# A graph layer over 64 samples: weights loaded on ScalarE's queue and combined between the first sample's products, and a third buffer for the token rows

## The chip, the cores and the metric

The kernel runs on one NeuronCore of a Trainium2 chip. TensorE (PE in the profile) multiplies matrices, VectorE (DVE), ScalarE (ACT) and GpSimd (POOL) work elementwise, and SyncE (SP) issues DMAs. Each engine takes its instructions in the order in which they were written, and waits at an instruction until what it needs is there. The metric is the device time of one execution in microseconds (us), lower is better. Times given are medians of several runs, beside one execution taken by the profiler.

## The reference

`x` holds 64 samples of 256 tokens by 768 features, `adj` 64 matrices of 256 by 256 with values 0 and 1. Cut to what matters, for each sample:

```python
h = relu((x - mean(x)) / sqrt(var(x) + 1e-5))
deg, rdeg = adj.sum(-1), adj.T.sum(-1)
ctx = adj @ (h @ Wadj.T + badj) / max(deg, 1)
ctx += adj.T @ (h @ Wrev.T + brev) / max(rdeg, 1)
ctx += h @ Wself.T + bself
rel = (adj-weighted sum of E[rels]) @ Wr.T + br * deg
rel += (the same, transposed) @ Wrr.T + brr * rdeg
out = x + ctx + rel
```

All of it is float32. The relation numbers are the entries of `adj` itself, so with entries 0 and 1 the sums over `E` reduce to one row of `E` times a degree. Should `adj` hold anything else, a general path behind a flag computes the sample again; with this input it isn't entered.

## The kernel before

**The products.** For one sample the left side has six blocks of 128 tokens by 768 features: `a0, a1, a2` for the first 128 tokens and `b0, b1, b2` for the last 128, where 0 is the aggregate over `adj`, 1 the aggregate over its transpose, and 2 the sample's own features. The right side has nine blocks of 768 by 256: `Wadj`, `Wrev` and `Wself` (first digit 0, 1, 2), each in three column blocks (second digit). Instead of the 18 block products, 15 are made, in the manner of fast matrix multiplication: `PRODUCTS` gives for each the combination of left blocks and of right blocks, and `ORDER` (line 62) the order in which they run, the PSUM bank each adds to, a row product that brings in the biases, which output blocks read the bank afterwards and with which sign, and which left combinations GpSimd has to form ahead. A product is six matmuls of 128x128 by 128x256 over the feature blocks (L333; the profile shows each as two instructions, x12 for a product), and five products have a row product behind them (L338), whose left side is `tokT`, the token rows of the sample: degrees and flags, transposed. Banks `x` and `y` have a buffer each; `w`, `z`, `v`, `u` and `t` take turns in two buffers of one pool, so that `z` of one step takes over the buffer that `t` of the step before had.

**The stages of a sample.** `load` brings in `x`, `adj` and the transposed `x` (three DMAs on SP). `degrees` converts `adj` on ScalarE and sums its rows. `statistics` gives mean, variance (VectorE, with the power -0.5 on GpSimd) and the degrees' reciprocals into `cols`. `spread` transposes `cols` on TensorE into `pt`; ScalarE copies it as `tokT` (L262) and as `line` (L264); `line` goes by two DMAs to DRAM (`d`) and comes back broadcast over all partitions as `row`. `normalise` makes `hx` on VectorE (L282), its upper part `hi` on ScalarE (L285) and the remainder `lo` on VectorE (L286), for each half of the tokens. `self_features` scales the transposed `x` by `row` in two GpSimd passes (L298) and takes its positive part on ScalarE (L299), which is left block 2. `aggregate` multiplies `hi` and `lo` with `adj` for one feature block (`pa`, L307), and VectorE scales the result into left blocks 0 and 1 (`X`, L312). `combine_left` (L328) forms a sum or difference of left blocks on GpSimd. `add_out` (L346 and L348) adds a bank to, or takes it from, the output that grows in the tile `x`, on VectorE.

**The order of the work.** Nothing is scheduled automatically: each engine's order is the order of the calls. `step(t)` (L350) runs the 15 products of sample M = t. Between them stand the six aggregates of A = t + 1 (after products 2 to 7) and its `self_features`, and for N = t + 2 the degrees and statistics (after the seventh), `spread` (after the tenth) and `normalise` (after the twelfth). At the end of the step GpSimd forms the first three left combinations of A, and the output of M leaves in one DMA of 768 KB.

**The buffers.** `tokT` comes from a pool of two (L261). `tokT` of N is written in step M after the tenth product, into the buffer of sample M, which the row products of M read up to the fifteenth.

**The start.** The steps -2 and -1 have no products. In step -2, after the loads of sample 0, `load_weights` (L150) issues 15 DMAs of 768 KB on SP, one weight block for each product; `prepare_rows` (L172) loads `eT`, `wr`, and the bias rows behind them on the same queue and builds `rows`, the right side of the row products; `combine_weights` (L156) makes the 15 sums and differences of weight blocks and two sign passes, all on VectorE. Only then does VectorE turn to sample 0's statistics.

**The end.** After the last step a sum over `others` and a tiny matmul give the flag (L398 to L401).

Of the kernel before, what the change touches and what calls it, by code (L numbers as in the profile page):

```python
# [9 lines left out]
F32 = mybir.dt.float32  # L10
F32R = mybir.dt.float32r
# [6 lines left out]
P = 128  # L18
# [4 lines left out]


PRODUCTS = {
    11: ("a1", "-12 +10 +22"),
    10: ("b2-a1", "+22 -11"),
    3: ("a1+b1", "+12 -02 -11"),
    2: ("a2+b2", "+21 -01 -22"),
    5: ("b0+b1", "+10"),  # L30
    9: ("a0+a2", "-20"),
    7: ("a1+a2", "+22"),
    8: ("a1+b0+b1", "+02 -10"),
    6: ("a0+a2+b2", "+20 -01"),
    15: ("b1+b2", "+11"),
    14: ("a0+a1+b0+b1", "-02"),
    12: ("a0+a2+b0+b2", "+01"),
    4: ("b2", "+21 -11 -20"),
    13: ("a0", "-00 +02 +20"),
    1: ("b0", "+00 -01 -10"),  # L40
}

# [12 lines left out]
}  # L55
AHEAD = ("b2-a1", "a1+b1", "a2+b2")

ROWS = ((0, 1, None), (1, 2, None), (0, None, 2), (0, 2, 0), (1, 1, None), (1, 0, 1))

# [10 lines left out]
    (8, "y", None, ((1, 1, 2),), ()),  # L70
    (6, "x", None, ((-1, 0, 1),), ("a0+a1+b0+b1",)),
    (15, "u", None, ((1, 1, 1, 2),), ("a0+a2+b0+b2",)),
    (14, "y", 2, ((-1, 0, 2),), ()),
    (12, "x", 4, ((1, 1, 1),), ()),
    (4, "t", None, ((-1, 0, 1), (1, 1, 1)), ()),
    (13, "y", 3, ((-1, 0, 0),), ()),
    (1, "x", 5, ((1, 1, 0),), ()),
)

# [2 lines left out]
def kernel(  # L82
# [54 lines left out]
    def main_path(main: ExitStack):  # L137
# [12 lines left out]
        def load_weights():  # L150
            for n, (_, right) in PRODUCTS.items():
                k, o = int(right[1]), int(right[2])
                v = (wadj_t, wrev_t, wself_t)[k].rearrange("(f p) o -> p f o", p=P)
                nc.sync.dma_start(W[n], v[:, :, ts(o, NB)])  # L154

        def combine_weights():  # L156
            single = {right[1:]: n for n, (_, right) in PRODUCTS.items() if len(right) == 3}
            for n, (_, right) in PRODUCTS.items():
                first, *others = right.split()
                for k, other in enumerate(others):  # L160
                    w = W[single[other[1:]]]
                    if other[0] == "-":
                        nc.vector.tensor_sub(W[n], W[n], w)  # L163
                    elif first[0] == "-" and k == 0:
                        nc.vector.tensor_sub(W[n], w, W[n])
                    else:
                        nc.vector.tensor_add(W[n], W[n], w)
            for block, n in single.items():
                if PRODUCTS[n][1][0] == "-":
                    nc.vector.tensor_scalar(W[n], W[n], -1.0, None, op0=ALU.mult)  # L170

        def prepare_rows():  # L172


            eT = pool1.tile([P, NREL], F32, name="eT")
            nc.sync.dma_start(eT, e_t)
            wr = [pool1.tile([P, H], F32, tag=f"hl{k}", name=f"wr{k}") for k in range(2)]
            nc.sync.dma_start(wr[0], wr_t)
            nc.sync.dma_start(wr[1], wrr_t)
            brow = pool3.tile([P, H], F32, tag="x", name="brow")  # L180
            nc.vector.memset(brow, 0.0)
            pick = pool1.tile([P, 2, P], F32, tag="t0", name="pick")
            nc.vector.memset(pick, 0.0)
            for q in range(4):
                nc.sync.dma_start(brow[q * 32 : q * 32 + NROW, :], bias)
                nc.vector.tensor_copy(pick[:, 0, q * 32 + 3 : q * 32 + 4], eT[:, 1:2])
                nc.vector.tensor_copy(pick[:, 1, q * 32 + 4 : q * 32 + 5], eT[:, NBASE + 1 : NBASE + 2])
            for n in range(2):
                pr = ps2.tile([P, 512], F32, tag="pa", name=f"pr{n}")
                for k in range(2):  # L190
                    nc.tensor.matmul(pr[:, :HO], pick[:, k, :], wr[k][:, ts(n, HO)], start=(k == 0), stop=(k == 1))
                nc.vector.tensor_add(brow[:, ts(n, HO)], brow[:, ts(n, HO)], pr[:, :HO])
            full = pool3.tile([P, len(ROWS), NB], F32, tag="x", name="rows_full")
            hi = pool1.tile([P, len(ROWS), NB], F32R, tag="hx", name="rows_hi")
            nc.vector.memset(full, 0.0)
            for q in range(4):
                at = slice(q * 32, (q + 1) * 32)
                for k, (c, plus, minus) in enumerate(ROWS):
                    if c != q // 2:
                        continue  # L200
                    if plus is None:
                        nc.vector.tensor_scalar(full[at, k, :], brow[at, ts(minus, NB)], -1.0, None, op0=ALU.mult)
                    elif minus is None:
                        nc.vector.tensor_copy(full[at, k, :], brow[at, ts(plus, NB)])
                    else:
                        nc.vector.tensor_sub(full[at, k, :], brow[at, ts(plus, NB)], brow[at, ts(minus, NB)])
            nc.vector.tensor_copy(hi, full)
            nc.vector.tensor_sub(rows, full, hi.bitcast(F32))
            for q in (0, 2):
                at = slice(q * 32, (q + 1) * 32)  # L210
                nc.vector.tensor_copy(rows[at], hi[at].bitcast(F32))

        S = [{} for _ in range(B)]

# [40 lines left out]
        def spread(b):  # L255

            s = S[b]
            v = cols[b % 2]
            pt = ps1.tile([P, P], F32, tag="pt", name=f"pt_{b}")
            nc.tensor.transpose(pt, v.rearrange("p c k -> p (c k)"), ident)  # L260
            s["tokT"] = pool2.tile([P, P], F32R, tag="tokT", name=f"tokT_{b}")  # L261
            nc.scalar.activation(s["tokT"], pt, AF.Copy)  # L262
# [6 lines left out]
            nc.sync.dma_start(  # L269
                s["row"].rearrange("p k i -> p (k i)"), d.rearrange("k c p -> (k c p)").partition_broadcast(P)  # L270
            )
# [68 lines left out]
        def add_out(b, ps, sign, c, n, many=1):  # L340
# [6 lines left out]
            else:  # L347
                nc.vector.tensor_sub(o, o, ps)  # L348

        def step(t):  # L350

            M, A, N = t, t + 1, t + 2
            has_m, has_a, has_n = 0 <= M < B, 0 <= A < B, 0 <= N < B
            if has_n:
                load(N)
            if t == -2:
                load_weights()
                prepare_rows()
                combine_weights()
            if has_a:  # L360
                new_left(A)
            banks = {}
            for k, (n, bank, row, reads, needs) in enumerate(ORDER):
                if has_m:
                    for name in needs:
                        combine_left(M, name)
                    start = bank not in banks
                    if start:
                        pool, tag = (ps1, bank) if bank in ("x", "y") else (ps2, "q")
                        banks[bank] = pool.tile([P, 512], F32, tag=tag, name=f"{bank}_{M}")[:, :NB]  # L370
                    product(M, n, banks[bank], start, row)
                    for read in reads:
                        add_out(M, banks[bank], *read)
# [15 lines left out]
            if has_m:  # L389
# [5 lines left out]
        for t in range(-2, B):  # L395
            step(t)
        total = pool1.tile([P, 1], F32, name="total")
        nc.vector.tensor_reduce(total, others, AX.X, ALU.add)  # L398
        pf = ps1.tile([P, P], F32, tag="pt", name="pf")
        nc.tensor.matmul(pf[:1, :1], total, ones[:, :1], start=True, stop=True)  # L400
        nc.vector.tensor_copy(flag, pf[:1, :1])  # L401

    def general_path(sub: ExitStack):

# [159 lines left out]
```

## Time and profile before

| | |
|---|---|
| median of 3 runs (lowest, highest) | 3280.49 us (3275.93, 3283.17) |
| profiled execution, its own time | 3272.29 us |
| its span, first to last instruction | 3270.5 us |
| mean granted TensorE clock | 0.975 of full |
| busy: TensorE, GpSimd, VectorE, ScalarE | 91%, 54%, 38%, 10% |
| mean DMA rate | 71 GB/s |

In the rows of the timeline and of the list of groups, `out<-in` are the names in the program; where one line records two instructions of a kind in a row, the count stands behind an x. PE is a matmul, PEld its weight load, SPq SyncE's queue of DMA issues. A row of the windows has, behind the stretch and its length, for PE, PEld, DVE, ACT and POOL the busy time and in brackets the number of instructions, then the granted TensorE clock as a share of full speed, the DMA engines' busy share, and GB/s. What stands as a releaser behind an arrow is what the waiting instruction waited for last.

### The profile page before, as it was taken

What the parts mean: (1) busy time and instruction counts of PE and PEld (TensorE: products, weight loads), DVE (VectorE), ACT (ScalarE), POOL (GpSimd) and SP (SyncE); (2) the same over time, 40 slices, a digit from 0 to 9 for tenths busy, and PEclk for the clock granted to TensorE, in tenths of its full rate; (3) what the DMA queues carried; (4) which work ended last, traced back from release to release, by engine and by line L of the source; (5) the groups of instructions that cost most, each with busy time, mean ns of one, the idle gap of its engine ahead of it and who ended that gap; (6) DMA issues with size and microseconds to landing.
All of it is one profiled execution on the core that took longest, in us unless ns stands there. A gap on an engine that the chain in (4) does not pass through costs nothing.

```text
span 3270.5 us, 33278 instructions
## 1 busy us (share of the span) xinstructions
PE 2972.6 (91%) x13514; PEld 2562.0 (78%) x13514; DVE 1235.7 (38%) x2550; ACT 340.1 (10%) x833; POOL 1771.5 (54%) x902
## 2 busy tenths in 40 slices
PE   0799999999999999999999999999999999999999
PEld 0687877877877877877877877878878778778777
DVE  4533343333333333333333333333333433433332
ACT  0110110110111111101101101101101101101100
POOL 0554654654654654655655655645645546546544
PEclk8899999999999999999999999999999999999999
DMA  5122122122122122222221221221221221221210
GB/s 181 66 83 74 52 84 75 52 75 81 54 75 77 59 75 68 68 74 68 68 75 58 78 75 58 78 74 56 80 74 52 84 75 52 83 75 52 78 65 21
DMA packets 125029, 233.25 MB, mean 71 GB/s; under 512 B 6068, under 2 KB 67252, under 8 KB 124872
## 3 DMA queue, kind: packets, MB, share of 16 engines
q1 hardware_dynamic: 124872, 231.08, 20.4%
q8 instruction: 109, 1.79, 0.2%
q14 instruction: 48, 0.39, 0.0%
HBM read 180.46 MB, written 50.59 MB: 71 GB/s over the span
## 4 chain that ended last, share of the span: by engine, by line
PE 86%; DVE 7%; ACT 4%; SPq 1%; issue 1%; DMA 0%; POOL 0%; ACTq 0%; POOLq 0%
PE y L333 20%; PE x L333 20%; PE z L333 12%; PE pa L307 11%; PE w L333 5%; PE u L333 5%; PE v L333 5%; PE t L333 5%; DVE lo L286 4%; ACT hi L285 3%; DVE hx L282 1%; SPq L154 1%; DVE x L346 1%; DVE x L348 1%; DVE w L163 1%
## 5 line engine op out<-in xcount | busy, mean ns | idle before, releaser
L328 POOL TENSOR_TENSOR b0+b<-X 128x768 f32<-128x768 f32 x64 | 117.2, 1831 | 988.0 <-PE z L333 988.0
L333 PE MATMUL y<-w,X 128*128 128x256 f32 x2304 | 528.6, 379 | 0.0
L333 PEld LDWEIGHTS y<-w,X 128*128 128x128 f32 x2304 | 432.5, 190 | 63.2
L298 POOL TENSOR_TENSOR xT<-xT,row 128x1536 f32<-128x1536 f32 x128 | 441.7, 3451 | 12.0 <-DMA row<-d 6.9
L333 PE MATMUL z<-w,b2-a 128*128 128x256 f32 x768 | 228.9, 460 | 194.2 <-DVE x L346 194.2
L333 PEld LDWEIGHTS z<-w,b2-a 128*128 128x128 f32 x768 | 170.6, 229 | 246.1 <-issue 217.3
L307 PE MATMUL pa<-a,hi 128*128 128x512 f32 x768 | 357.1, 465 | 2.1 <-ACT hi L285 2.1
L328 POOL TENSOR_TENSOR X<-X 128x768 f32<-128x768 f32 x192 | 350.1, 1824 | 10.9 <-PE y L333 5.9
L333 PE MATMUL x<-w,a2+b 128*128 128x256 f32 x1536 | 352.4, 379 | 0.0
L333 PE MATMUL x<-w,X 128*128 128x256 f32 x1536 | 352.3, 379 | 0.0
L312 DVE TENSOR_TENSOR X<-pa,row 128x512 f32<-128x512 f32 x384 | 265.8, 692 | 184.1 <-PE pa L307 182.7
L286 DVE SCALAR_TENSOR_TENSOR lo<-hx,cols,hi 128x768 fp32r<-128x768 f32 x128 | 130.4, 1018 | 507.0 <-ACT hi L285 507.0
L333 PEld LDWEIGHTS x<-w,X 128*128 128x128 f32 x1536 | 286.8, 190 | 40.3
L333 PEld LDWEIGHTS x<-w,a2+b 128*128 128x128 f32 x1536 | 287.2, 190 | 38.0
L307 PE MATMUL pa<-a,lo 128*128 128x512 f32 x768 | 305.1, 397 | 0.5 <-DVE lo L286 0.5
L299 ACT ACTIVATE X<-xT 128x1536 f32<-128x1536 f32 x64 | 95.5, 1491 | 1482.0 <-POOL xT L298 1482.0
L328 POOL TENSOR_TENSOR a2+b<-X,a2+b 128x768 f32<-128x768 f32 x128 | 231.5, 1809 | 1.6 <-PE x L333 1.6
L243 POOL TENSOR_TENSOR cols<-cols,half 128x2 f32<-128x2 f32 x64 | 69.0, 1078 | 236.9 <-DVE cols L242 236.9
L328 POOL TENSOR_TENSOR a2+b<-X 128x768 f32<-128x768 f32 x64 | 115.9, 1811 | 118.4 <-PE x L338 118.4
L333 PE MATMUL w<-w,X 128*128 128x256 f32 x768 | 178.7, 383 | 0.0
L328 POOL TENSOR_TENSOR a1+a<-X 128x768 f32<-128x768 f32 x64 | 117.1, 1830 | 109.3 <-PE w L338 109.3
L333 PE MATMUL t<-w,X 128*128 128x256 f32 x768 | 176.3, 379 | 0.0
(86 smaller groups left out, 4055.3 us busy)
## 6 DMA issues: line engine op xcount, KB each, us to landing
x<-in_x_dram SPq DMA_DIRECT2D x64, 768.0 KB
xT<-in_x_t_dram SPq DMA_DIRECT2D x64, 768.0 KB
out_dram<-x SPq DMA_DIRECT2D x64, 768.0 KB
adj<-in_adj_dram SPq DMA_DIRECT2D x64, 512.0 KB
row<-d SPq DMA_DIRECT2D x64, 512.0 KB
w<-in_Wself_dram SPq DMA_DIRECT2D x6, 768.0 KB
w<-in_Wadj_dram SPq DMA_DIRECT2D x5, 768.0 KB
w<-in_Wrev_dram SPq DMA_DIRECT2D x4, 768.0 KB
```

The source lines that it names most:

```text
L154: nc.sync.dma_start(W[n], v[:, :, ts(o, NB)])
L163: nc.vector.tensor_sub(W[n], W[n], w)
L243: nc.gpsimd.tensor_tensor(v[:, :, RSTD], v[:, :, RSTD], half, op=ALU.pow)
L282: nc.vector.tensor_scalar(hx[:, c, :], s["x"][:, c, :], v[:, c, MEAN : MEAN + 1], 0.0, op0=ALU.subtract, op1=ALU.max)
L285: nc.scalar.activation(s["hi"][:, c, :], hx[:, c, :], AF.Copy, scale=rstd)
L286: nc.vector.scalar_tensor_tensor(s["lo"][:, c, :], hx[:, c, :], rstd, s["hi"][:, c, :].bitcast(F32), op0=ALU.mult, op1=ALU.subtract)
L298: nc.gpsimd.tensor_tensor(xT, xT, row[:, k : k + 1, :].to_broadcast([P, F, L]), op=op)
L299: nc.scalar.activation(s["X"][:, :, 2, :], xT, AF.Relu)
L307: nc.tensor.matmul(pa, s[part][:, c, ts(f, P)], s["a"][:, c, :, :].rearrange("p s i -> p (s i)"), start=(k == 0), stop=(k == 2 * C - 1),)
L312: nc.vector.tensor_mul(s["X"][:, f, 0:2, :].rearrange("p s i -> p (s i)"), pa, s["row"][:, 2:4, :].rearrange("p s i -> p (s i)"))
L328: nc.gpsimd.tensor_tensor(L[name], L[x], L[y], op=op)
L333: nc.tensor.matmul(ps, l[:, f, :], W[n][:, f, :], start=(start and f == 0), stop=(row is None and f == F - 1), skip_group_check=not start,)
```

## The change

Five things change. The weights are loaded on ScalarE's queue instead of SP's. A function `start()` replaces the steps -2 and -1: it writes the whole front of sample 0 first, with the weights' DMAs between its degrees and its statistics, then the combinations of the weights of the first product, the bias rows, the weights of the next two products, and the statistics and normalisation of sample 1. The other combinations stand in step 0, each three products ahead of its use. The bias rows' loads move ahead of the weights (`load_rows`), their fills go to GpSimd and two conversions to ScalarE; the row pieces are written 64 partitions at a time. `tokT` has three buffers. Signs in `PRODUCTS`, `ORDER` and `ROWS` are turned so that a weight block that is stored negated is negated once (`turn`, on ScalarE) ahead of its first use. The output leaves in two halves, the first after the fourteenth product, and the flag is computed inside the last step. The arithmetic of a steady step is the same, but for signs.

```diff
-    5: ("b0+b1", "+10"),
+    5: ("b0+b1", "-10"),
...
-    (5, "y", None, ((1, 1, 0),), ("a0+a2",)),
+    (5, "y", None, ((-1, 1, 0),), ("a0+a2",)),
...
-                nc.sync.dma_start(W[n], v[:, :, ts(o, NB)])
...
+                nc.scalar.dma_start(W[n], v[:, :, ts(o, NB)])
+
+        single = {right[1:]: n for n, (_, right) in PRODUCTS.items() if len(right) == 3}
+        turned = set()
+
+        def turn(n):
+
+            if PRODUCTS[n][1][0] == "-" and n not in turned:
+                nc.scalar.activation(W[n], W[n], AF.Copy, scale=-1.0)
+                turned.add(n)
+
+        def combine_weights(n):
+
+            first, *others = PRODUCTS[n][1].split()
+            if not others:
+                turn(n)
+            for k, other in enumerate(others):
+                m = single[other[1:]]
+                turn(m)
+                if other[0] == PRODUCTS[m][1][0]:
+                    if first[0] == "-" and k == 0:
+                        nc.vector.tensor_sub(W[n], W[m], W[n])
                     else:
...
+                        nc.vector.tensor_add(W[n], W[n], W[m])
+                else:
+                    assert first[0] == "+" or k > 0
+                    nc.vector.tensor_sub(W[n], W[n], W[m])
...
+        def load_rows():
...
+            nc.gpsimd.memset(brow, 0.0)
...
+            nc.gpsimd.memset(pick, 0.0)
+            R["full"] = pool2.tile([P, len(ROWS), NB], F32, tag="X", name="rows_full")
+            nc.gpsimd.memset(R["full"], 0.0)
...
-            nc.vector.tensor_copy(hi, full)
+            nc.scalar.activation(hi, full, AF.Copy)
             nc.vector.tensor_sub(rows, full, hi.bitcast(F32))
...
-            s["tokT"] = pool2.tile([P, P], F32R, tag="tokT", name=f"tokT_{b}")
+            s["tokT"] = pool3.tile([P, P], F32R, tag="tokT", name=f"tokT_{b}")
...
+        def start():
+
+            load(0)
+            load_rows()
+            degrees(0)
+            load_weights()
+            statistics(0)
+            spread(0)
+            normalise(0)
+            load(1)
+            new_left(0)
+            self_features(0)
+            for f in range(F):
+                aggregate(0, f)
+            left_blocks(0)
+            for name in AHEAD:
+                combine_left(0, name)
+            combine_weights(ORDER[0][0])
+            prepare_rows()
+            for k in (1, 2):
+                combine_weights(ORDER[k][0])
+            degrees(1)
+            statistics(1)
+            spread(1)
+            normalise(1)
...
+                for name in needs:
+                    combine_left(M, name)
+                if t == 0 and k + 3 < len(ORDER):
+                    combine_weights(ORDER[k + 3][0])
...
+                if t == B - 1 and k == 2:
+                    flag_others()
+                if k == 13:
+                    nc.sync.dma_start(out_v[M][:, 0, :], S[M]["x"][:, 0, :])
...
-            if has_m:
-                nc.sync.dma_start(out_v[M], S[M]["x"])
+            nc.sync.dma_start(out_v[M][:, 1, :], S[M]["x"][:, 1, :])
```

How this moves instructions is shown at three places. The number behind a tile's name is its buffer, the line numbers of the changed kernel are its own, and the weight tiles `w_88` to `w_102` are those of products 11, 10, 3, 2, 5, 9, 7, 8, 6, 15, 14, 12, 4, 13 and 1.

ScalarE at the start, before, from the degrees of sample 0:

```order
L230 ACTIVATE a_199,tok_104<-adj_114 128x256 x4
L262 ACTIVATE tokT_221<-pt_219 128x128
L264 ACTIVATE line_223<-pt_219 128x128
L285 ACTIVATE hi_230<-hx_232,cols_106 128x768 x2
L299 ACTIVATE X_245<-xT_116 128x6x256
L230 ACTIVATE a_285,tok_105<-adj_241 128x256 x4
L262 ACTIVATE tokT_307<-pt_305 128x128
```

ScalarE at the same place now, from the last two of the 15 weight DMAs, which follow the degrees of sample 0:

```order
L154 DMA w_101<-in_Wadj_dram 128x6x256
L154 DMA w_102<-in_Wadj_dram 128x6x256
L274 ACTIVATE tokT_171<-pt_169 128x128
L276 ACTIVATE line_173<-pt_169 128x128
L297 ACTIVATE hi_180<-hx_182,cols_106 128x768 x2
L311 ACTIVATE X_195<-xT_116 128x6x256
L162 ACTIVATE w_92<-w_92 128x1536
L219 ACTIVATE rows_hi<-rows_full 128x1536
L223 ACTIVATE rows<-rows_hi 32x1536 x2
L242 ACTIVATE a_268,tok_105<-adj_191 128x256 x4
```

The weight DMAs now stand between the degrees and the `tokT` copy, and a sign pass and the rows' conversions between sample 0's features and sample 1's degrees.

VectorE behind the aggregates of sample 0, before:

```order
L312 TENSOR_TENSOR X_245<-pa_3_264,row_228 128x512
L312 TENSOR_TENSOR X_245<-pa_4_270,row_228 128x512
L312 TENSOR_TENSOR X_245<-pa_5_279,row_228 128x512
L240 BN_STATS stats_290<-x_239 128x6 x2
L241 BN_AGGR cols_107<-stats_290 128x2
```

The same place now, up to the first pieces of the bias rows:

```order
L324 TENSOR_TENSOR X_195<-pa_5_229,row_178 128x512
L175 TENSOR_TENSOR w_88<-w_94,w_88 128x1536
L180 TENSOR_TENSOR w_88<-w_88,w_92 128x1536
L205 COPY pick<-eT 128x4 x2
L210 TENSOR_TENSOR brow<-brow,pr_246 128x384
L210 TENSOR_TENSOR brow<-brow,pr_250 128x384
L216 COPY rows_full<-brow 64x256 x2
L218 TENSOR_TENSOR rows_full<-brow 64x256
```

Between the aggregates of sample 0 and the statistics of sample 1 now stand the first weights' combinations and the whole building of the bias rows, followed by the three combinations for products 10 and 3. All of these stood ahead of sample 0's statistics.

VectorE in step 0, behind the third aggregate of sample 1, before:

```order
L312 TENSOR_TENSOR X_337<-pa_2_386,row_314 128x512
L346 TENSOR_TENSOR x_112<-x_112,y_393 128x256
L312 TENSOR_TENSOR X_337<-pa_3_401,row_314 128x512
L348 TENSOR_TENSOR x_112<-x_112,x_409 128x256
L312 TENSOR_TENSOR X_337<-pa_4_417,row_314 128x512
```

And now:

```order
L324 TENSOR_TENSOR X_314<-pa_2_366,row_297 128x512
L180 TENSOR_TENSOR w_95<-w_95,w_98 128x1536
L360 TENSOR_TENSOR x_112<-x_112,y_374 128x256
L324 TENSOR_TENSOR X_314<-pa_3_382,row_297 128x512
L180 TENSOR_TENSOR w_96<-w_96,w_99 128x1536
L360 TENSOR_TENSOR x_112<-x_112,x_391 128x256
L324 TENSOR_TENSOR X_314<-pa_4_399,row_297 128x512
```

Each weight combination stands ahead of the read of a bank and of the scaling of an aggregate, which wait behind it on VectorE.

More of the change, by code (lines that the diff above doesn't have):

```diff
@@ L153, in load_weights @@
                 v = (wadj_t, wrev_t, wself_t)[k].rearrange("(f p) o -> p f o", p=P)
[L154 to L165, printed above, removed]
-                    else:
[L167 to L183, printed above, removed]
+                nc.scalar.dma_start(W[n], v[:, :, ts(o, NB)])
@@ L363, in step @@
             for k, (n, bank, row, reads, needs) in enumerate(ORDER):
-                if has_m:
[L365 to L373, printed above, removed]
+                for name in needs:
+                    combine_left(M, name)
+                if t == 0 and k + 3 < len(ORDER):
+                    combine_weights(ORDER[k + 3][0])
+                start = bank not in banks
+                if start:
+                    pool, tag = (ps1, bank) if bank in ("x", "y") else (ps2, "q")
+                    banks[bank] = pool.tile([P, 512], F32, tag=tag, name=f"{bank}_{M}")[:, :NB]
+                product(M, n, banks[bank], start, row)
+                for read in reads:
+                    add_out(M, banks[bank], *read)
                 if has_a and k in (1, 2, 3, 4, 5, 6):
@@ L394, in main_path @@
             nc.vector.memset(cols[i], 0.0)
-        for t in range(-2, B):
+        start()
+        for t in range(B):
             step(t)
[L397 to L401, printed above, removed]
     def general_path(sub: ExitStack):
```

62 lines of the change are left out of this document (34 added, 28 removed).

## The prediction

> **What bounds the kernel now.** The page comes first: TensorE is busy nearly all the time, so only its own pauses and what lies ahead of its first product can shrink.
>
> ```profile
> span 3270.5 us, 33278 instructions
> PE 2972.6 (91%) x13514; PEld 2562.0 (78%) x13514; DVE 1235.7 (38%) x2550; ACT 340.1 (10%) x833; POOL 1771.5 (54%) x902
> ```
>
> The profiled execution took 3272.29 us, 1.79 over its span; the three timed runs have a median of 3280.49. Then the list of waits (us in total, times, longest): whom does TensorE wait for, and who is held in the same rhythm?
>
> ```profile
> ACT tokT L262 <- PE x L338: 1183.5, 62, 19.1
> PE z L333 <- DVE x L346: 194.2, 62, 3.3
> ```
>
> Both waits come 62 times, once a sample. 194.2 us is TensorE's only large pause, 194.2/62 = 3.13 us a step. The timeline around the turn of one step shows how the two hang together (start, us, engine, line, what; in brackets the idle time before).
>
> ```profile
> 1086.33 0.27 PE L260 MATMUL pt<-ident,cols 128*128 128x128 f32 x1
> 1092.05 1.81 POOL L328 TENSOR_TENSOR a2+b<-X 128x768 f32<-128x768 f32 x1 [1.87 <-PE x L338]
> 1092.40 1.88 DVE L282 TENSOR_SCALAR hx<-x,cols 128x768 f32<-128x768 f32 x1
> 1099.56 0.47 PE L338 MATMUL x<-rows,tokT 128*128 128x256 f32 x1
> 1099.87 2.75 PE L333 MATMUL w<-w,X 128*128 128x256 f32 x12
> ...
> 1100.07 0.28 ACT L262 ACTIVATE tokT<-pt 128x128 fp32r<-128x128 f32 x1 [19.09 <-PE x L338]
> 1100.40 0.94 ACT L285 ACTIVATE hi<-hx,cols 128x768 fp32r<-128x768 f32 x1
> 1101.37 1.02 DVE L286 SCALAR_TENSOR_TENSOR lo<-hx,cols,hi 128x768 fp32r<-128x768 f32 x1 [7.09 <-ACT hi L285]
> 1102.31 0.61 DVE L282 TENSOR_SCALAR hx<-x,cols 128x768 f32<-128x768 f32 x1
> 1102.95 0.93 ACT L285 ACTIVATE hi<-hx,cols 128x768 fp32r<-128x768 f32 x1 [1.62 <-DVE hx L282]
> 1103.92 1.02 DVE L286 SCALAR_TENSOR_TENSOR lo<-hx,cols,hi 128x768 fp32r<-128x768 f32 x1 [1.00 <-ACT hi L285]
> 1105.19 0.41 DVE L346 TENSOR_TENSOR x<-x,t 128x256 f32<-128x256 f32 x1
> 1105.75 2.83 PE z L333 x12
> ```
>
> The transpose `pt` of sample N is done at 1086.6, but ScalarE copies it into `tokT` only at 1100.07, when the last row product of the running sample (1099.56, L338) has read the same buffer: two buffers, three samples alive. ScalarE's `hi` queues behind the copy, VectorE's `lo` waits 7.09 us for `hi`, and VectorE takes nothing out of order, so the reads of bank `t` come after both halves of `lo`. Product 10 (`z`) needs that bank's buffer and starts at 1105.75, 3.1 us late.
>
> The pause costs more than itself. In the windows, the granted clock is 0.63 where `z` follows a pause, and 1.00 over 31 us without one:
>
> ```profile
> 1055.40:1060.00 4.60, 4.54 (x13) 3.76 (x14) 0.91 (x3) 0.00 (x0) 0.00 (x0) 0.63 0.45 175
> 1120.00:1151.00 31.00, 31.00 (x147) 27.00 (x145) 11.69 (x26) 4.35 (x12) 18.14 (x9) 1.00 0.08 26
> ```
>
> The chain of waits, with one row of the timeline, gives step lengths from `z` to `z`:
>
> ```profile
> 165.85 4.21 PE z L333 x12
> 1055.46 4.51 PE z L333 x12
> 3180.96 2.83 PE z L333 x12
> 3226.16 2.75 PE L333 MATMUL z<-w,b2-a 128*128 128x256 f32 x12
> ```
>
> From step 1's `z` (165.85) to step 62's (3180.96) are 61 steps of 49.43 us. From 1055.46 to 1105.75, with a slow `z`, 50.29. From step 62's to step 63's (3226.16), with no pause at its end because nothing is normalised any more, 45.20.
>
> **Steady state.** The third `tokT` buffer lets ScalarE copy at 1086.6. What is late next? `hi` then waits for `hx`, which ends at 1092.40 + 1.88 = 1094.3. In the rows, the reads of `t` end 5.2 us after `hi` starts (1100.40 to 1105.60). So they end at 1099.5, while product 11 (`w`) keeps TensorE until about 1102.6: 3.1 us to spare, and no pause left. GpSimd stays where it is, relative to TensorE's products, and its last piece there (1092.05) is over before `lo` begins. I take 45.35 for a step: 45.20 plus 0.15 for the transpose that step 62 lacks. Bounds are 45.20 and 45.47 (1055.46 to 1105.75 less 3.13 and less the slow product's surplus, 4.51 - 2.83). So 61 x (49.43 - 45.35) = 249 us go, and 3.1 before step 1's `z`.
>
> The Trainium skill, "TensorE: Matmul & The Clock Gate", What's actually happening, has the clock halved after an idle window of about 3.4 us. By that a pause of 3.13 would cost no clock, and the buffer would give only the 194 us of pauses (rival E). The trace says otherwise: the 0.63 stands right behind a pause, and the mean of 49.43 lies halfway between 50.29 and 50.29 - 1.68, so about every other step pays.
>
> **The front.** Rows of the first 112 us, and the window that has the DMA rate in its last column:
>
> ```profile
> 2.26 0.92 SPq L154 DMA_DIRECT2D w<-in_Wrev_dram  x1
> 9.41 0.19 ACT L230 ACTIVATION_READ_ACCUMULATOR a<-adj 128x1 f32 x1
> 29.92 4.75 SPq L154 DMA_DIRECT2D w<-in_Wadj_dram  x2
> 43.94 5.45 PE L191 MATMUL pr<-wr,pick 128*128 128x384 f32 x8 [43.94 <-DMA wr<-in_Wr_dram]
> 59.72 1.76 DVE L165 TENSOR_TENSOR w<-w,w 128x1536 f32<-128x1536 f32 x1
> 87.25 1.01 DVE L240 BATCH_NORM_STATS2 stats<-x 128x6 f32<-128x384 f32 x2
> 91.48 0.47 PE L260 MATMUL pt<-ident,cols 128*128 128x128 f32 x1 [42.09 <-POOL cols L243]
> 91.99 0.28 ACT L262 ACTIVATE tokT<-pt 128x128 fp32r<-128x128 f32 x1 [82.39 <-PE pt L260]
> 94.00 0.35 SPq L269 DMA_DIRECT2D row<-d  x1
> 98.36 7.07 POOL L298 TENSOR_TENSOR xT<-xT,row 128x1536 f32<-128x1536 f32 x2 [6.94 <-DMA row<-d]
> 103.79 0.69 DVE L312 TENSOR_TENSOR X<-pa,row 128x512 f32<-128x512 f32 x1 [0.22 <-PE pa L307]
> 105.46 1.48 ACT L299 ACTIVATE X<-xT 128x1536 f32<-128x1536 f32 x1 [9.66 <-POOL xT L298]
> 108.09 1.80 POOL L328 TENSOR_TENSOR b2-a<-X 128x768 f32<-128x768 f32 x1
> 108.58 1.33 DVE L249 TENSOR_SCALAR tok<-tok 128x4 f32<-128x4 f32 x1 [0.99 <-ACT a L230]
> 112.07 5.33 PE L333 MATMUL w<-w,X 128*128 128x256 f32 x12
> ```
>
> ```profile
> 10.00:50.00 40.00, 5.45 (x8) 2.35 (x8) 1.69 (x10) 0.00 (x0) 0.00 (x0) 1.00 0.93 301
> ```
>
> Before, the first sample waits for 15 weight combinations on VectorE (59.72 to 87.25) and those for the bias rows, whose loads stand behind 11.8 MB of weights. Products start at 112.07. After, walking the new orders:
>
> 1. GpSimd's three fills and SP's other loads are issued in the first microseconds, beside the degrees' wait for their input. ScalarE has the degrees done at 9.6, then issues 15 weight loads ahead of the `tokT` copy. On SP the issues took from 2.26 to 34.67, 32.4 us, held to the pace at which data moved. The same bytes stand ahead of the last one, plus `eT` and the two `wr` (0.83 MB, 2.7 us at 301 GB/s), so ScalarE is free at about 38. Bounds: 15 x 0.92 after 9.6 gives 23.4, 32.4 after 9.6 gives 42.0. VectorE's statistics lie under this.
> 2. From the `tokT` copy to the landing of `row` took 91.99 to 98.3, 6.3 us; the last weights share the engines, for which I add 2 (0 to 6): 46.3.
> 3. `xT` on GpSimd 7.07, `Relu` 1.48: 54.9. The aggregates and their `X` (last at 103.79, 5.5 us after the landing) lie beside that.
> 4. The sign turn of weight 5 on ScalarE queues behind the `Relu`, another 128x1536 pass: 1.48, then the second combination for product 11, 1.76: 58.1.
> 5. The `pick` copies meet GpSimd's three left combinations. At 108.58 a 128x4 instruction took 1.33 and ended at 109.9, when the GpSimd operation of 108.09 did (+1.80); I add 2.4 (0 to two such, 3.6): 60.5.
> 6. The `pr` products 5.45: 66.0. Building the rows took 49.4 to 59.72 before; the fill is now on GpSimd, the pieces are half as many, the casts are on ScalarE: 6 (5 to 10.3): 72.0.
> 7. Sample 1's loads stand on SP behind `row`, as before, and land some 25 us ahead of this. Three combinations at 1.76, statistics of sample 1 up to the transpose as from 87.25 to 91.48, and the transpose that TensorE has ahead of product 11: 5.3 + 4.2 + 0.5 = 82.0.
>
> So the first product comes at 82.0, 30.1 earlier. The turned signs in the tables exchange additions for subtractions of the same shape; the two sign passes leave VectorE for ScalarE, the second (weight 9) beside products 11 to 5. Step 0 took 165.85 - 112.07 = 53.8, less the 3.1 of pause. Ten combinations now run inside it or just ahead, on VectorE, between reads that TensorE needs. Without interference 17.6 us fit beside a step's TensorE time; with it, each may wait for a GpSimd operation of 1.8, 18 in all. I take 4, nearer the lower end because the banks are double. The Trainium skill, "SBUF — State Buffer", SBUF: two separate sides, says that a VectorE instruction with two SBUF inputs and a GpSimd instruction that reads SBUF lock each other out for their whole length, which speaks for the upper end; the 108.58 row agrees for a one-input instruction, no row shows it for a combination, since all of them lie ahead of GpSimd's first product of the front at 98.36.
>
> **The tail.**
>
> ```profile
> 3263.93 0.19 PE L400 MATMUL pf<-ones,total 128*1 128x1 f32 x2 [0.64 <-DVE total L398]
> ```
>
> The last output DMA carries 384 KB less, 1.3 us at 301 GB/s. The flag product waited 0.64 us for its sum at the end, beside that DMA; now TensorE meets this wait inside step 63, with the read ahead of it about 1 us. I count 0 for both. The output's two halves queue on SP behind `row` of a sample that is needed a step later, and ahead only of loads that wait for them anyway.
>
> **The sum.** 82.0 + 50.7 + 4 = 136.7 for step 1's `z`; 61 x 45.35 = 2766.4; from step 62's `z` to the end 3270.5 - 3180.96 = 89.5. Span 2992.6, with 1.79 more 2994.4, against 3272.29. The median lies 8.2 above the profiled execution; part of that should be the pauses' changing cost in clock, so I add 4: 2998.
>
> **Rivals.**
> A. A wait takes the place of the old one: `hi` starts later than I read, and `t` is read late again. For: `hx` at 1092.40 took 1.88 behind a GpSimd piece, against 0.61 at 1102.31. Against: 3.1 us of room. With half of the pause left, 62 x 1.56 = 97: 3095. Chance 0.08.
> B. The front gains nothing, since ScalarE is held by the weight issues beyond 42 and `row` crawls among the weights; products start at 112 as before: 2998 + 30 = 3028, with step 0's 18 instead of 4 up to 3042. Chance 0.06.
> C. The token wait isn't removed (ScalarE held by something else up to the same product): only the front's 26: 3280 - 26 = 3254. Chance 0.03.
> D. Slower: TensorE without pauses is granted less clock for the whole run. 63 steps of 45.35 are 2857 us, the rest is 141. The time passes 3280 when the clock falls under 2857/3139 = 0.91; at 0.85 it would be 3502. Against: 1.00 in the 31 us window. Chance 0.04.
> E. The slow `z` isn't the pause's doing, and stays: 2998 + 58 = 3056. For: nothing but the rule above. Against: 45.20 where there was no pause. Chance 0.02.
>
> **How the numbers follow.** My forecast has 0.76, and 0.01 lies below its range. Low: ScalarE free at 23.4 (-15), step 0 undisturbed (-4), 45.20 a step (-9), not all of it: 2972. High: 42.0 (+4), `row` (+4), the rows (+4), step 0 (+14), 45.47 (+7), and a median as far above as before (+4): 3035, which takes in most of B. Within 0.2% (6.6 us, about what a measurement here can tell) only the edge of D lies: 0.01; slower 0.03; faster 0.96.
>
> **What would show it.** The wait of `tokT` for L338's successor is gone from the list, and TensorE's for the `t` read is near 0; `z` to `z` is 45.2 to 45.5 in all steps; the first product is at 75 to 90, with ScalarE's last weight issue near 38; step 0's `z` to `z` is longer than a steady step by some us. The prediction is wrong if TensorE still waits every step, or if the steps are even but longer than 46.

## The result and the profile after

The changed kernel takes 2993.76 us (median of 4 runs, 2992.76 to 2994.13), the kernel before 3278.21 in the same comparison (3269.48 to 3283.17). The ratio is 0.9134, with a 95% interval of 0.9114 to 0.9155. The profiled execution took 2993.87 us, with a span of 2992.0.

The page of the changed kernel, its span and busy times:

```profile
span 2992.0 us, 33451 instructions
PE 2911.9 (97%) x13514; PEld 2533.5 (85%) x13514; DVE 1243.4 (42%) x2530; ACT 355.3 (12%) x838; POOL 1779.5 (59%) x905
```

TensorE's busy time fell by 61 us although it has as many instructions as before, 13514. Of that, 52.7 us are in the product `z` (228.9 us busy before, 176.2 now), which ran in part at a lower clock. The list of waits after (us in total, times, longest):

```profile
ACT tokT L274 <- PE pt L272: 355.9, 63, 5.7
DVE lo L298 <- ACT hi L297: 161.7, 128, 28.1
PE y L345 <- DVE x L358: 2.5, 1, 2.5
```

The copy into `tokT` now waits only for its input, the transpose, and no longer for the row product. `lo` waits 161.7 us instead of 507.0, 28.1 of them once, in the front. TensorE's wait of 62 times 3.1 us for the reads of bank `t` is gone; the longest that it has among the products is 2.5 us, once, in step 0. The turn of a steady step, in the timeline of the changed kernel:

```profile
1031.57 0.28 ACT L274 ACTIVATE tokT<-pt 128x128 fp32r<-128x128 f32 x1 [5.70 <-PE pt L272]
...
1037.33 1.88 DVE L294 TENSOR_SCALAR hx<-x,cols 128x768 f32<-128x768 f32 x1
...
1040.30 1.02 DVE L298 SCALAR_TENSOR_TENSOR lo<-hx,cols,hi 128x768 fp32r<-128x768 f32 x1 [1.09 <-ACT hi L297]
...
1043.79 0.41 DVE L360 TENSOR_TENSOR x<-x,t 128x256 f32<-128x256 f32 x1
1044.12 0.41 DVE L358 TENSOR_TENSOR x<-x,t 128x256 f32<-128x256 f32 x1
...
1047.39 2.75 PE L345 MATMUL z<-w,b2-a 128*128 128x256 f32 x12
```

`tokT` is copied at 1031.57, `lo` follows `hx` by the length of `hi`, and the reads of `t` end at 1044.53, 2.9 us ahead of `z` at 1047.39. `z` takes 2.75 us (2.78 in step 1). A window of 1000 us shows the clock (first number behind the brackets) at 1.00:

```profile
1000.00:2000.00 1000.00, 1000.00 (x4666) 872.37 (x4664) 414.64 (x860) 119.24 (x286) 608.32 (x308) 1.00 0.22 77
```

Step 1's `z` and step 62's, from the timeline of TensorE, give the step length:

```profile
142.43 2.78 PE L345 MATMUL z<-w,b2-a 128*128 128x256 f32 x12
2902.50 2.75 PE L345 MATMUL z<-w,b2-a 128*128 128x256 f32 x12
```

(2902.50 - 142.43) / 61 = 45.25 us, against 49.43. The front of the changed kernel, rows of its timeline up to the first product:

```profile
33.44 4.38 ACTq L154 DMA_DIRECT2D w<-in_Wadj_dram  x2
37.87 0.28 ACT L274 ACTIVATE tokT<-pt 128x128 fp32r<-128x128 f32 x1 [27.87 <-DMA w<-in_Wadj_dram]
...
38.34 0.59 SPq L279 DMA_DIRECT2D d<-line  x2
...
43.28 0.35 SPq L281 DMA_DIRECT2D row<-d  x1
...
48.39 7.05 POOL L310 TENSOR_TENSOR xT<-xT,row 128x1536 f32<-128x1536 f32 x2 [39.06 <-DMA row<-d]
...
60.25 4.88 PE L209 MATMUL pr<-wr,pick 128*128 128x384 f32 x8 [4.87 <-DVE pick L205]
...
65.27 1.80 POOL L340 TENSOR_TENSOR b2-a<-X 128x768 f32<-128x768 f32 x1 [9.84 <-PE pr L209]
65.76 3.27 DVE L216 COPY rows_full<-brow 64x256 f32<-64x256 f32 x2
...
68.95 2.01 DVE L218 TENSOR_TENSOR rows_full<-brow 64x256 f32<-64x256 f32 x1
...
75.10 5.21 DVE L180 TENSOR_TENSOR w<-w,w 128x1536 f32<-128x1536 f32 x3
...
84.73 4.52 PE L345 MATMUL w<-w,X 128*128 128x256 f32 x12
```

ScalarE issues its last weight up to 37.82 and copies `tokT` behind it; `row` lands at 48.3; the first product starts at 84.73 instead of 112.07.

### The profile page after: what moved, and what is told of

It reads as the page before. It is cut to its first block, busy times and chain, and to the rows that moved or that the text cites. A ratio compares the mean times of both kernels' runs of the same rounds, so it can differ in the third digit from the quotient of the medians.

```text
span 2992.0 us, 33451 instructions
## 1 busy us (share of the span) xinstructions
PE 2911.9 (97%) x13514; PEld 2533.5 (85%) x13514; DVE 1243.4 (42%) x2530; ACT 355.3 (12%) x838; POOL 1779.5 (59%) x905
## 4 chain that ended last, share of the span: by engine, by line
PE 96%; DVE 1%; POOL 1%; ACTq 1%; DMA 1%; ACT 0%; issue 0%; SPq 0%; POOLq 0%
PE y L345 22%; PE x L345 22%; PE pa L319 12%; PE w L345 11%; PE z L345 11%; PE t L345 5%; PE u L345 5%; PE v L345 5%; ACTq L154 1%; POOL xT L310 1%; PE y L350 1%; PE x L350 0%; DVE w L180 0%; PE w L350 0%; PE z L350 0%; PE pt L272 0%
## 5 line engine op out<-in xcount | busy, mean ns | idle before, releaser
L319 PEld LDWEIGHTS pa<-a,hi 128*128 128x128 f32 x768 | 146.4, 191 | 61.3 <-ACT hi L297 29.6
L298 DVE SCALAR_TENSOR_TENSOR lo<-hx,cols,hi 128x768 fp32r<-128x768 f32 x128 | 130.4, 1019 | 161.7 <-ACT hi L297 161.7
L297 ACT ACTIVATE hi<-hx,cols 128x768 fp32r<-128x768 f32 x128 | 119.9, 937 | 563.3 <-DVE hx L294 563.3
L345 PE MATMUL w<-w,a1+b 128*128 128x256 f32 x768 | 176.3, 379 | 0.9 <-DVE x L360 0.9
```

The source lines that it names most:

```text
L297: nc.scalar.activation(s["hi"][:, c, :], hx[:, c, :], AF.Copy, scale=rstd)
L298: nc.vector.scalar_tensor_tensor(s["lo"][:, c, :], hx[:, c, :], rstd, s["hi"][:, c, :].bitcast(F32), op0=ALU.mult, op1=ALU.subtract)
L319: nc.tensor.matmul(pa, s[part][:, c, ts(f, P)], s["a"][:, c, :, :].rearrange("p s i -> p (s i)"), start=(k == 0), stop=(k == 2 * C - 1),)
L345: nc.tensor.matmul(ps, l[:, f, :], W[n][:, f, :], start=(start and f == 0), stop=(row is None and f == F - 1), skip_group_check=not start,)
```

## The experiments

Nine kernels were run, each compared with the kernel before on the same chip. Medians are of 4 or 5 runs. Where two of the nine, or one of them and the changed kernel, differ by a few us, the places in their traces are compared.

### The third buffer alone

```diff
-            s["tokT"] = pool2.tile([P, P], F32R, tag="tokT", name=f"tokT_{b}")
+            s["tokT"] = pool3.tile([P, P], F32R, tag="tokT", name=f"tokT_{b}")
```

> The kernel before with the third token row buffer alone. My theory: the front stays (first product near 112 us), step 1's z comes 3.1 us earlier, at 162.7, and all steps are of 45.25 us as in the changed kernel: 162.7 + 61 x 45.25 + 89.5 = span 3012, time 3014. Rival E (the slow z is not the pause's doing): 58 us more, 3072. Rival (the steady gain comes from another edit, such as the split output): 3272 as before.

Measured: 3012.60 us, ratio 0.9197 (0.9181 to 0.9212). Step 1's `z` and step 62's:

```profile
161.85 2.75 PE L333 MATMUL z<-w,b2-a 128*128 128x256 f32 x12
2921.49 2.75 PE L333 MATMUL z<-w,b2-a 128*128 128x256 f32 x12
```

The steps are of 45.24 us, within 0.01 of those of the changed kernel. One word in one line brings 264 of the 284 us. Rival E, that the slow `z` would stay, falls.

### All but the third buffer

```diff
-            s["tokT"] = pool3.tile([P, P], F32R, tag="tokT", name=f"tokT_{b}")
+            s["tokT"] = pool2.tile([P, P], F32R, tag="tokT", name=f"tokT_{b}")
```

This edit is made to the changed kernel.

> The changed kernel with two token row buffers as before. My theory: only the front is better; first product at 84.7, step 1's z at 145.6, then steps of 49.4 with the pause of 3.1 in each: 145.6 + 61 x 49.43 + 89.5 = span 3250, time 3252. Rival (the other edits bear part of the steady gain): steps under 49 us and a time well below 3240.

Measured: 3261.89 us, ratio 0.9954 (0.9938 to 0.9970). The waits show the old pause in full:

```profile
ACT tokT L274 <- PE x L350: 1188.7, 62, 22.9
PE z L345 <- DVE x L358: 194.3, 62, 3.3
```

Mean step 49.56 us. The other edits, taken together, don't shorten a steady step. The time is 10 us above what I expected, 8 of them in the steps (61 x 0.13).

### Two buffers, but the reads of `t` ahead of the normalisation

```diff
-                if has_n and k == 11:
+                if has_n and k == 14:
                     normalise(N)
```

> The kernel before with two token buffers, but with the normalisation of the next sample behind the last product's read instead of behind the twelfth product, so that VectorE reads bank t before it meets the wait for hi. My theory (the pause is VectorE's order, and the buffer only one way out of it): ScalarE still waits some 19 us for the token buffer, but TensorE no longer pauses; steps of 45.3, time 3014 to 3020. Rival (the buffer itself is what TensorE lacks, or hi and lo then come too late for the aggregates): pauses move to the aggregates, 1 to 3 us a step, 3075 to 3270.

Measured: 3027.46 us, ratio 0.9240 (0.9225 to 0.9256). ScalarE's wait is as long as ever, and TensorE's is gone from the list:

```profile
ACT tokT L262 <- PE x L338: 1183.2, 62, 19.1
```

The timeline at the turn of a step:

```profile
1068.84 0.42 DVE L346 TENSOR_TENSOR x<-x,x 128x256 f32<-128x256 f32 x1 [2.29 <-PE x L338]
...
1070.88 1.02 DVE L286 SCALAR_TENSOR_TENSOR lo<-hx,cols,hi 128x768 fp32r<-128x768 f32 x1 [1.08 <-ACT hi L285]
...
1071.23 2.75 PE L333 MATMUL z<-w,b2-a 128*128 128x256 f32 x12
```

`z` starts on time at 1071.23 while `lo` is still under way. Steps are of 45.48 us, 0.24 above those with three buffers: `hi` and `lo` now end so late that the aggregates run right behind them (their weight loads wait 17.7 us for `lo` in all, 0.28 a step). So the buffer as such was never what TensorE lacked. It lacked VectorE, which stood in line behind ScalarE's wait.

### A longer pause

```diff
+        scratch = pool1.tile([P, 768], F32, name="scratch")
...
                 if has_n and k == 11:
                     normalise(N)
+                    for _ in range(2):
+                        nc.vector.memset(scratch, 0.0)
```

> The kernel before with two fills of a scratch tile on VectorE behind each normalisation, about 1.3 us, so the pause ahead of z grows from 3.1 to about 4.4 us. If the clock falls only after an idle stretch that just about matches the pause, every step now pays with a slow z: 51.3 us a step, time 3391. If the share of steps that pay stays at a half: 50.7 us a step, time 3353. If the slow z has nothing to do with the pause's length, it too stays at a half.

Measured: 3452.73 us, ratio 1.0538 (1.0520 to 1.0556), slower than either expectation. TensorE's wait ahead of `z`, in the list of waits:

```profile
PE z L335 <- DVE x L348: 298.0, 62, 5.0
```

And one slow `z`, in the timeline:

```profile
1058.14 5.46 PE L335 MATMUL z<-w,b2-a 128*128 128x256 f32 x12 [4.80 <-DVE x L348]
```

The pause grew to 298.0/62 = 4.81 us, 0.4 more than I gave the fills. All 62 `z` behind it are slow (over 3.5 us), where it was 30 of 62 before, and many take 5.46 us instead of 4.51. A step takes 52.35 us. Beyond 45.25 and the pause of 4.81 that is 2.29 us; the next experiment shows how much of it is clock.

### A shorter pause

```diff
                 if has_n and k == 11:
-                    normalise(N)
+                    normalise(N, (0,))
+                if has_n and k == 12:
+                    normalise(N, (1,))
```

`normalise` takes the halves of the tokens that it is to work on; nothing else in it changes.

> The kernel before with two token buffers, normalising the second half of the next sample only behind the reads of bank t, so that these wait for one half of lo instead of two. My theory (what TensorE waits for is the reads of t behind lo): the pause ahead of z shrinks from 3.1 to about 0.6 us, and up to 1 us appears at the aggregates; if a pause under 1 us costs no clock, steps of 46.0 to 46.8 us, time 3060 to 3108. Rival (any pause costs about the same in clock): 1 us a step more, up to 3170.

Measured: 3065.26 us, ratio 0.9342 (0.9328 to 0.9356).

The same wait, and a `z` behind it:

```profile
PE z L335 <- DVE x L348: 36.0, 62, 0.7
```

```profile
1039.36 2.83 PE L335 MATMUL z<-w,b2-a 128*128 128x256 f32 x12 [0.57 <-DVE x L348]
```

The pause is 36.0/62 = 0.58 us, `z` takes 2.83 us in each of the 62 steps, and a step 46.08 us. That is 0.25 us more than 45.25 and the pause, and none of it is clock, which a window over nearly the whole run shows at 1.00:

```profile
118.30:3060.00 2941.70, 2903.21 (x13468) 2509.11 (x13466) 1169.19 (x2459) 329.66 (x807) 1755.93 (x889) 1.00 0.21 73
```

The three pauses together, with TensorE's busy time in the 64 products `z` (176.2 us without pauses):

| pause ahead of `z` | step | beyond 45.25 and the pause | busy in `z` | slow `z` |
|---|---|---|---|---|
| 0.58 us (split) | 46.08 us | 0.25 us | 181.2 us | 0 of 62 |
| 3.13 us (before) | 49.43 us | 1.05 us | 228.9 us | 30 of 62 |
| 4.81 us (longer) | 52.35 us | 2.29 us | 303.0 us | 62 of 62 |

By the slow `z`, the clock costs (228.9 - 181.2)/62 = 0.77 us a step behind the pause of 3.13 us and (303.0 - 181.2)/62 = 1.96 us behind that of 4.81. The rest, about 0.3 us, is for the most part there without any loss of clock too, as the split shows with its 0.25.

The length alone doesn't say which pauses pay. In the kernel before they are all of 3.12 to 3.31 us, and slow and fast `z` take turns for most of the run. Two neighbours, and the windows behind the first:

```profile
215.83 4.51 PE L333 MATMUL z<-w,b2-a 128*128 128x256 f32 x12 [3.13 <-DVE x L346]
...
266.12 2.83 PE L333 MATMUL z<-w,b2-a 128*128 128x256 f32 x12 [3.12 <-DVE x L346]
```

```profile
216.43:219.84 3.41, 3.41 (x10) 2.71 (x9) 0.25 (x1) 0.00 (x0) 0.00 (x0) 0.50 0.61 235
219.84:315.42 95.58, 89.33 (x416) 77.36 (x415) 37.14 (x78) 10.57 (x26) 55.32 (x28) 1.00 0.19 64
```

The clock is halved for 3.41 us, and next from 315.42 on, 98.99 us or 29 such lengths later. Each trace holds the times at which the granted clock changed, and in each of them they lie on one even grid of 3.41 us, which runs on whatever the kernel does; a piece of the grid is the time between two of its marks. What decides is how a pause falls on it. The first pause, 212.70 to 215.83, fills 2.81 us of the piece from 213.02 to 216.43, and the piece behind it is at half clock. The second, 263.00 to 266.12, is cut by the grid at 264.22 into 1.22 and 1.90 us, and nothing follows. So it goes for all 186 pauses of this kind in the traces of the kernel before, of all but the third buffer and of the longer pause, and for the 62 of the split: the 124 that fill 2.02 us or more of one piece are followed by half clock, the others, with 2.00 us at most, are not. The 4.81 us always fill at least 2.70.

The Trainium skill, "TensorE: Matmul & The Clock Gate", What's actually happening, names an idle window of about 3.4 us that runs freely. The traces agree with its length and with its running freely, but not with its having to be idle as a whole: about 2 of the 3.41 us were enough.

### The weights on SP's queue, at the same place

```diff
-                nc.scalar.dma_start(W[n], v[:, :, ts(o, NB)])
+                nc.sync.dma_start(W[n], v[:, :, ts(o, NB)])
```

This and the next two edits are made to the changed kernel.

> The changed kernel with the weight DMAs back on SP's queue, at the same place in the program. My theory (the weights' bytes set the pace, and d and row come behind them on either queue): ScalarE makes hi at 11 us instead of 38, but row lands within 2 us of 48.3, the first product stays at 83 to 87, time 2994 within 4. Rival (ScalarE's hold is what the front waits for): first product some 10 us or more earlier, 2984 or less. Rival (a second queue lets row pass the weights): row lands 5 us later or more, 2999 or more.

Measured: 2996.31 us, ratio 0.9134 (0.9121 to 0.9146), where the changed kernel had 2993.76 in its own comparison. ScalarE copies `tokT` at once, but `d` and `row` stand behind the weights on SP:

```profile
10.90 0.28 ACT L274 ACTIVATE tokT<-pt 128x128 fp32r<-128x128 f32 x1 [1.18 <-PE pt L272]
...
37.67 2.47 SPq L279 DMA_DIRECT2D d<-line  x2
...
46.10 0.35 SPq L281 DMA_DIRECT2D row<-d  x1
...
86.07 4.24 PE L345 MATMUL w<-w,X 128*128 128x256 f32 x12
```

The first product comes 1.3 us later than with the weights on ScalarE's queue. Of the change, the second queue is worth that little here. On SP's queue 27 us of ScalarE's time are freed and nothing is gained, because `d` and `row` come behind the issues of the weights either way: here on the queue itself, in the changed kernel because `tokT` and `line` wait on ScalarE.

### The weights behind the first sample's `row`

```diff
             degrees(0)
-            load_weights()
             statistics(0)
             spread(0)
+            load_weights()
             normalise(0)
```

The weights go on SP's queue here, as in the experiment before.

> The changed kernel with the weight DMAs on SP's queue behind the row DMA of sample 0, so that the first sample's front runs to its end without them. My theory (the row's late landing is what starts the chain of the front): row lands near 18 us instead of 48.3, the combinations then wait for the seventh and later weights, landing from 33 us on, the first product comes near 62 and the time falls by 20 to 25 to about 2971. Rival (the weights' landing sets the front): first product at 75 or later, 2985 or more.

Measured: 2970.85 us (2970.54 to 2971.22), ratio 0.9056 (0.9043 to 0.9068), some 23 us below the changed kernel. `row` is issued at 12.88 and used at 17.22, and the first combination waits 8.96 us for a weight:

```profile
12.88 0.35 SPq L281 DMA_DIRECT2D row<-d  x1
...
17.22 7.06 POOL L310 TENSOR_TENSOR xT<-xT,row 128x1536 f32<-128x1536 f32 x2 [8.22 <-DMA row<-d]
...
33.17 1.76 DVE L175 TENSOR_TENSOR w<-w,w 128x1536 f32<-128x1536 f32 x1 [8.96 <-DMA w<-in_Wself_dram]
...
61.64 4.65 PE L345 MATMUL w<-w,X 128*128 128x256 f32 x12
```

The first product comes at 61.64. Against the experiment before, only the place of the weights differs. What the front had waited for was the landing of `row`.

### All combinations in the front

```diff
-            for k in (1, 2):
+            for k in range(1, len(ORDER)):
                 combine_weights(ORDER[k][0])
...
-                if t == 0 and k + 3 < len(ORDER):
-                    combine_weights(ORDER[k + 3][0])
```

> The changed kernel with all weight combinations in the front, none between the products of step 0. My theory (between the products they cost step 0 the 7 us by which it is longer than a steady step, in the front they would cost their full 17.6 us): first product near 102, step 0 near 50.5, time 3004. Rival (step 0 is longer for other reasons, the cold clock and the first loads): step 0 stays near 57, time 3011.

Measured: 3002.69 us, ratio 0.9153 (0.9140 to 0.9165). The first product and step 1's `z`:

```profile
101.81 4.45 PE L345 MATMUL w<-w,X 128*128 128x256 f32 x11
151.57 2.75 PE L345 MATMUL z<-w,b2-a 128*128 128x256 f32 x12
```

Step 0 lasts 49.76 us from one to the other, against 142.43 - 84.73 = 57.70 in the changed kernel. So the combinations between the products cost step 0 7.9 us and save 17.1 in the front: 9 us net, the measured difference.

### The bias rows earlier

```diff
+            prepare_rows()
             left_blocks(0)
             for name in AHEAD:
                 combine_left(0, name)
             combine_weights(ORDER[0][0])
-            prepare_rows()
```

This edit is made to the kernel with the weights behind `row`.

> The kernel with the weights behind the row DMA, and the building of the bias rows moved ahead of the first weight combination, into the time in which VectorE waits for the weights' landing. My theory (in the front VectorE's chain of rows, combinations and statistics is what the first product waits for): the rows are done at about 38 us, the combinations at 50, sample 1's statistics then wait for its x behind the weights, first product near 55 instead of 61.6, time about 2964. Rival (the weights and sample 1's loads set the time): first product at 60 or later, 2969 or more.

Measured: 2967.22 us (2967.04 to 2967.42), ratio 0.9052 (0.9040 to 0.9065), the lowest median of all. The interval overlaps with that of the kernel it was made from, 3.6 us above; the trace shows the same 3.6 us in the first product, 58.07 instead of 61.64. The 58.07 are 3 us later than I expected: sample 1's statistics wait 4.89 us for its `x`, which stands behind the weights on SP.

```profile
53.56 1.02 DVE L252 BATCH_NORM_STATS2 stats<-x 128x6 f32<-128x384 f32 x2 [4.89 <-DMA x<-in_x_dram]
...
58.07 4.16 PE L345 MATMUL w<-w,X 128*128 128x256 f32 x12
```

So both named causes act, one behind the other: VectorE's chain until it is moved, then the loads.

## Why the prediction was right

The span was forecast at 2992.6 us and came out at 2992.0. That closeness is luck: the terms were off by up to 7 us, in both directions.

**The steady state** was right in mechanism and a little too long. The step that VectorE's reads are freed by the third buffer, and that no other wait follows at once, is shown by the buffer alone, by all but the buffer, and by the reversed order with two buffers. That a pause costs clock, for which the prediction had only one window and step lengths, is shown by the longer and the shorter pause. "About every other step pays" was right for the reason that the grid of 3.41 us gives, which the prediction didn't know; of the 1.05 us a step that it would put down to the clock, 0.77 are. A step took 45.25 us, inside the bounds of 45.20 to 45.47 and 0.10 below the value taken: 61 x 0.10 = 6.3 us. The slack of 3.1 us ahead of `z` measured 2.9. Rivals A, C, D and E fall with these steps and the clock of 1.00, B with the first product at 84.73.

**The front** was right up to ScalarE's last weight, 2 us short at `row`, and too short again behind `pr`. ScalarE free at 38: 37.87. `row` landed at 48.3 instead of 46.3. The 2 us added for sharing the DMA engines were half of what it took: `d` and `row` together took from 38.34 to 48.3, 10 us, against 5.8 before (92.46 to 98.3).

**The wrong step of the front** is the fifth. I let the `pick` copies wait behind GpSimd's left combinations; `pr` then began at 60.25, where the 60.5 forecast held only because `row` was 2 us late. In fact it went the other way round: the left combinations go into the tiles in which `wr` and `pick` lay, so GpSimd waited 9.8 us for the `pr` matmuls. Its three operations (65.27 to 70.7) then met the row pieces on VectorE: two copies took 3.27 us and one subtraction 2.01, as the rows above show; the like pieces right behind, when GpSimd had ended, took 0.50 and 0.42. The sixth step's 6 us became 10 (65.1 to 75.1), near its upper end. The first product was 2.7 us late in sum.

**Step 0** paid 7.9 us, not 4, for ten combinations; without them it took 49.76 us, where the prediction had 50.7, so that it ended 3 us later in sum. The rows of the changed kernel show VectorE and GpSimd taking turns:

```profile
120.47 1.82 POOL L340 TENSOR_TENSOR b2-a<-X 128x768 f32<-128x768 f32 x1
...
121.12 2.78 DVE L180 TENSOR_TENSOR w<-w,w 128x1536 f32<-128x1536 f32 x1
...
122.24 3.32 POOL L340 TENSOR_TENSOR a1+b<-X 128x768 f32<-128x768 f32 x1
...
123.93 3.25 DVE L177 TENSOR_TENSOR w<-w,w 128x1536 f32<-128x1536 f32 x1
...
132.64 4.54 PE L345 MATMUL y<-w,X 128*128 128x256 f32 x12 [2.49 <-DVE x L358]
```

A combination that takes 1.76 us alone takes 2.78 or 3.25, a GpSimd operation of 1.82 takes 3.32, and each ends some 1.6 us behind the other's end. That is what the Trainium skill, "SBUF — State Buffer", SBUF: two separate sides, says of two inputs in SBUF, and what no row of a combination could show before; the trace agrees. I had taken 4 out of a range of 0 to 18, and 7.9 is still in its lower half. The product at 132.64 waits 2.5 us for a read that stands behind combinations on VectorE, and behind this pause the product takes 4.54 us, another slow one.

**The end** took 89.5 us from step 62's `z`, as forecast, and as much with the buffer alone (3011.0 - 2921.49): the output in halves and the earlier flag gained nothing there.

**The sum.** Steady state: 259.5 us by the span with the third buffer alone (3270.5 to 3011.0), forecast 252. Front and step 0: 161.85 - 142.43 = 19.4 from the start of step 1's `z` with the buffer alone, forecast 26. Both miss by about 7 us, in opposite directions.

**The median** was not 4 us above the profiled execution but 0.1 below it. The kernel before spreads over 13.7 us from run to run, the changed one over 1.4. The prediction put part of the distance down to the pauses' changing cost in clock; all of it went with the pauses. The clock listed for each run bears this out. In the nine runs of the kernel before that stand beside the last experiment, no longer run has a higher clock than a shorter one; it goes from 0.975 in the shortest (3271.36 us) to 0.970 in the longest (3284.11). With pauses of 4.81 us, which always pay, it is 0.950 in all four runs, and they lie within 2.7 us. How the pauses fell on the grid of 3.41 us in the runs without a trace isn't on record, so that this is where the clock differs stays argued.

## What to carry to other kernels

When an engine waits briefly in every round, follow the engine that releases it to what it was doing, and that one to what it waited for: here TensorE, VectorE, ScalarE, and then a buffer of 64 KB that was still being read. A pause of a few microseconds on TensorE can cost a quarter to two fifths as much again in clock (0.77 us behind 3.13, 1.96 behind 4.81), and shortening it to 0.58 us saved that part too. Loads that the first work doesn't need belong behind those that it does; moving them to another queue, ahead of those, gained 1 us here, putting them behind 25.

## What the runs showed of the hardware that was not expected

The cost of a pause in clock isn't a fixed amount: nothing behind 0.58 us, 0.77 on average behind 3.13, 1.96 behind 4.81. A pause paid when it filled 2.02 us or more of one piece of a grid of 3.41 us, and not when it filled 2.00 or less, in all 248 pauses looked at. A slow `z` took up to 5.46 us, about twice its 2.75, where the half clock lay over the whole product.

The issue of `d` in the timeline of the kernel before (`row` at 94.00 stands in the prediction):

```profile
92.46 0.59 SPq L267 DMA_DIRECT2D d<-line  x2
```

From the issue of the two small DMAs `d` to the issue of `row`, which waits for them, it took 4.9 us while weight loads were in flight on the other queue (38.34 to 43.28), 1.5 us without such loads (92.46 to 94.00 before), and 8.4 us behind them on the same queue (37.67 to 46.10).
